# A four-block decoder in one launch: VectorE's links, biases, divisions and norms given to ScalarE and GpSimd, and the first entry's keys sent another way

## The chip, the cores and the metric

The kernel runs on one core of a Trainium2 chip. A core has TensorE (matrix multiplication, PE in the profile, with PEld for its weight loads), VectorE (DVE), ScalarE (ACT), GpSimd (POOL) and SyncE (SP), which here issues nearly all DMAs. The metric is the device time of one execution, in microseconds. Three runs of the kernel before gave 2719.85, 2715.16 and 2719.38 us; their median is 2719.38.

## The reference

Four sequences of 512 rows by 128 features go through twelve layers, each followed by an addition and a layer norm. Every block is a self-mixing layer, an attention across to a context of 154 rows, and a feed-forward layer.

```python
def _layernorm(x, axis=-1, eps=1e-05):
    m = jnp.mean(x, axis=axis, keepdims=True)
    v = jnp.var(x, axis=axis, keepdims=True)
    return (x - m) / jnp.sqrt(v + eps)

x = _layernorm(x + L0_attn(x))            # 16 heads of 8, rotary positions, biases
x = _layernorm(x + L0_xattn(ctx, x))      # own layer norm inside, gamma, beta, biases
x = _layernorm(x + L0_ffn(x))
x = _layernorm(x + L1_attn(x))            # a state scan
x = _layernorm(x + L1_xattn(x, ctx, ctx, mask))
x = _layernorm(x + L1_ffn(x))             # mixture of experts
x = _layernorm(x + L2_attn(x))            # causal attention
x = _layernorm(x + L2_xattn(x, ctx, ctx)) # no mask, biases
x = _layernorm(x + L2_ffn(x))
x = _layernorm(x + L3_attn(x))            # 16 heads of 8, no biases
x = _layernorm(x + L3_xattn(x, ctx, ctx, mask))
x = _layernorm(x + L3_ffn(x))
```

Each attention is the usual one:

```python
scores = jnp.einsum('bhqd,bhkd->bhqk', q, k) / jnp.sqrt(jnp.float32(d_k))
p = jax.nn.softmax(scores, axis=-1)
x = jnp.einsum('bhqk,bhkd->bhqd', p, v)
```

## The kernel before

**Attention with two passes over the scores.** The layers L0_attn and L3_attn (`self_attention`, L605) and the four cross attentions (`cross_attention`, L815) share a scheme. Scores are first computed with queries on the partitions, and VectorE takes their maxima (L671 in self attention, 128 x 2 from 128 x 1024; L962 in cross attention, 128 x 4 from 128 x 616). GpSimd splits a negated maximum into three bfloat16 parts (`split_maxima`, L493 to L496: four small instructions). TensorE transposes these parts (pmx, L504), and the *link* (L506) puts them into the rows of the query operand that are kept for them. Then the scores are computed again, with keys on the partitions (st at L683, stx at L957): the operand's extra rows subtract the maximum within the multiplication. ScalarE takes exp of them, straight from PSUM (L692, L968), and TensorE multiplies by the values (av, avx). So a unit of four heads goes: scores, maxima, split, pmx, link, scores again, exp, values.

**Operands in parts.** A query or key in float32 is carried as three bfloat16 parts in 64 rows of an operand qP or kP: six blocks of 8 rows for products of parts, and rows for maxima. `send` (L403) makes them: projection on TensorE (ps_proj, L407), bias and scale into `raw` (L409, L411 or L413), split into `part` on GpSimd (L414 to L417), and six writes on SP's queue to an area in HBM, far_q, far_k or far_kc (L421), which spread the parts over the rows. `arrive` (L479) loads the operand from there with two DMAs (L482). `raw` and `part` have one buffer each per pool, so one send follows another through them. Rows from `SLOT` on hold the maxima, and the key's rows there are constants, written once by `other_rows` (L278).

**Who makes a bias.** Self attention's query and key biases go through ScalarE (`scaled_bias`, L411). All other biases go through VectorE (L413), which reads the projection in PSUM: cross attention's keys (128 x 154) and queries (128 x 512).

**The order of the work.** Layers are generators, and a list by hand says after which step of a layer a piece goes (`agenda`). A unit of self attention has eight half steps; the first pass runs LEAD = 6 steps ahead of the second. Queries and keys of the next layer are sent from within the present one, where `new["room"]` is set: after steps with s % 16 in (7, 10, 13), L768. For L0_attn and L3_attn this includes s = 61, near their end, where the query of entry 2 of the following cross attention is sent. The first entry's keys in L0_attn use the same raw and part as its query, VectorE makes their parts, and their writes and loads stand on SP's queue behind those of the query.

**Cross attention.** `step(n)` (L1037) does in order: a half step (scores of unit n + 2, second scores of unit n), `sums(n - 1)`, `link_maxima(n + 1)`, the agenda, another half step, `more_sums(n - 1)`, `left(n)` for the last 26 keys, `split_maxima(n + 2)`. PSUM tiles of one bank (pmx, stx, sl, pto and others) come from one ring of three. L0_xattn is the one with `shuffled`: its output is transposed by VectorE (ot, L1011), divided there (rec, L1013, and zt, L1014), gets the input added and a norm of its own (`inner`, `outer`, L1030), where GpSimd applies gamma, beta and the residual. L1_xattn and L3_xattn have a mask, L0_xattn and L2_xattn have none.

**Norms.** `ln_stats` (L329) takes means and variances on VectorE, `applied` (L344) subtracts and scales with four tensor_scalar of 128 x 128 on VectorE (L346).

Of the kernel before, what the change touches and what calls it, by code (L numbers as in the profile page):

```python
# [21 lines left out]
P = 128  # L22
B, S, D = 4, 512, 128
NT = S // P
# [150 lines left out]
def decoder_kernel(ctx: ExitStack, tc: tile.TileContext, x, ctxT, mask1, mask3, packs, offsets, out, layers):  # L175
# [102 lines left out]
    def other_rows(far, what, n):  # L278
        for r in range(2):
            nc.sync.dma_start(far[r, 48:, :, :], flat[:, what : what + 1, :n].to_broadcast([16, 8, n]))  # L280
# [63 lines left out]
    def applied(dst, ys, n, mv, rs):  # L344
        for t in range(n):
            nc.vector.tensor_scalar(  # L346
                dst[:, t, :], ys[:, t, :], mv[:, t, 0:1], rs[:, t : t + 1], ALU.subtract, ALU.mult
            )
# [43 lines left out]
    def scaled(what, scale, pool, name):  # L392
        if scale == 1.0:
            return what
        t = pool.tile([P, 1], F32, name=name, bufs=1)
        nc.vector.tensor_scalar(t, what, scale, None, ALU.mult)
        return t


    Q_ROWS, K_ROWS = ((0, 1, 3), (3, 2, 2), (4, 1, 1)), ((2, 1, 3), (1, 4, 2), (0, 1, 1))  # L400
    SLOT = 48

    def send(far, order, w, rhs, scale, bias, raw, part, scaled_bias=None, on=nc.gpsimd):  # L403

        n = rhs.shape[-1]
        pj = psum_t("ps_proj", kind="a" if "a" in ring else "t")
        nc.tensor.matmul(pj[:, :n], lhsT=w, rhs=rhs, start=True, stop=True)  # L407
        if bias is None:
            nc.scalar.activation(raw, pj[:, :n], AF.Copy, scale=scale)  # L409
        elif scaled_bias is not None:  # L410
            nc.scalar.activation(raw, pj[:, :n], AF.Identity, bias=scaled_bias, scale=scale)  # L411
        else:
            nc.vector.tensor_scalar(raw, pj[:, :n], bias, scale, ALU.add, ALU.mult)  # L413
        on.tensor_copy(part[:, 0, :], raw)  # L414
        on.tensor_tensor(raw, raw, part[:, 0, :], ALU.subtract)
        on.tensor_copy(part[:, 1, :], raw)
        on.tensor_tensor(part[:, 2, :], raw, part[:, 1, :], ALU.subtract)  # L417
        for i, (at, by, m) in enumerate(order):
            for r in range(2):
                rows = far[r].rearrange("(s k) p c -> (k p) s c", k=DK)  # L420
                nc.sync.dma_start(  # L421
                    rows[:, at : at + by * (m - 1) + 1 : by, :],
                    part[64 * r : 64 * r + 64, i : i + 1, :].to_broadcast([64, m, n]),
                )
# [41 lines left out]
    class Operands:  # L466
# [12 lines left out]
        def arrive(self, dst, far):  # L479

            for p in (slice(0, 2), slice(2, 8)):
                nc.sync.dma_start(dst[:, p, :], far.rearrange("r q p c -> (r q) p c")[:, p, :])  # L482
# [15 lines left out]
        def link_maxima(self, n):  # L498

            pm = psum_t("pmx", (P, 2, S), BF16, "a")  # L500
            nm = self.nm[n % 2].rearrange("p (t g) k -> p t (g k)", t=NT)
            for i in range(2):
                for qt in range(NT):
                    nc.tensor.transpose(pm[:, i, qt * P : (qt + 1) * P], nm[:, qt, i * P : (i + 1) * P], identb)  # L504
            q = self.q[n // 4 % 2][:, 2 * (n % 4) : 2 * (n % 4) + 2, :]
            nc.vector.tensor_tensor(q, q, pm, ALU.add)  # L506
# [18 lines left out]
    def out_pieces(b, o, w, keep, cur, new, last, split=False):  # L525
# [23 lines left out]
        return [turn_over, times] + finish_pieces(b, ys, new, last, split)  # L549

    def finish_pieces(b, ys, new, last, split=False):
# [3 lines left out]
        def norm():  # L555
            if split:
                applied(xs, ys, NT, *stats)
            else:
                normed(xs, ys, NT, "f")
            if last:  # L560
                nc.sync.dma_start(out[b].rearrange("(t p) d -> p t d", p=P), xs)
# [43 lines left out]
    def self_attention(w, source, q_scale, k_scale, room, keep, pool, cur, new, last):  # L605
# [5 lines left out]
        bqs = scaled(w["bq"], q_scale, pool, "bqs") if "bq" in w else None  # L611
# [5 lines left out]
        def prepare(b):  # L617
# [21 lines left out]
            def queries():  # L639
                far = far_q[cur["index"] % 2][b]  # L640
                if ("q", b) not in cur["sent"]:
                    send(far, Q_ROWS, w["wq"], src, q_scale, bqs, *room_to_send(pool, S), scaled_bias=bqs)
                ops.arrive(m["q"], far)

            def keys():
                if ("k", b) not in cur["sent"]:

                    on = nc.vector if cur["index"] == 0 and b == 0 else nc.gpsimd
                    send(
                        far_k[b], K_ROWS, w["wk"], src, k_scale, w.get("bk"), *room_to_send(pool, S),  # L650
                        scaled_bias=w.get("bk"), on=on,
                    )
# [44 lines left out]
        def sums(s, h):  # L697
# [17 lines left out]
            if kt == NT - 1:  # L715
# [3 lines left out]
                if j == 3:  # L719
                    pieces = out_pieces(b, m["o"], w, keep, cur, new, last, split=True)  # L720
# [40 lines left out]
        for s in range(steps + LAG):  # L761
# [6 lines left out]
            new["room"] = (lambda n: room_to_send(pool, n)) if s % 16 in (7, 10, 13) else None  # L768
# [46 lines left out]
    def cross_attention(w, cur, new, last, room, scale, mask=None, shuffled=False):  # L815
# [179 lines left out]
        def more_sums(n):  # L995
# [18 lines left out]
            nc.vector.tensor_tensor(  # L1014
# [3 lines left out]
            if j == 3:  # L1018
# [9 lines left out]
                def outer():  # L1028
                    applied(ys, zt, NT, *stats)
# [6 lines left out]
        def step(n):  # L1036
# [5 lines left out]
            if 0 <= n + 1 < units:  # L1042
                ops.link_maxima(n + 1)
# [1361 lines left out]
```

## Time and profile before

| What | Value |
|---|---|
| median of three runs | 2719.38 us |
| the profiled execution's own time | 2717.01 us |
| its span, first to last instruction | 2715.2 us |
| mean granted TensorE clock | 0.959 |
| TensorE busy | 2445.9 us, 90% |
| VectorE busy | 1705.6 us, 63% |
| ScalarE busy | 1240.4 us, 46% |
| GpSimd busy | 1043.7 us, 38% |
| the link, L506, 96 times | 65.7 us, 684 ns each |
| a norm's part, L346, 128 x 128, 188 times | 71.4 us, 447 ns each on the mean |

All times in the profile count from the span's start. L0_attn runs to about 250 us, L0_xattn to 365, L1_attn's scan from 580 to 860, L1_xattn to 980, L2_xattn from 1860 to 1960, L3_attn from 2100 to 2306, L3_xattn to 2430. In a line of the groups, the first number after the bar is the sum of busy time in us, the second the mean of one in ns, and behind the second bar stands idle time of the engine before these instructions, with what ended it. In a line of the timeline stand start in us, duration in us, engine, line, operation, output and input, the count, and in brackets the idle time before it and what ended that.

### The profile page before, as it was taken

To read this page: it belongs to the slowest core of one execution; us is meant where nothing else is said; L and a number is where in the kernel's file an instruction comes from. 1 tells how busy PE (TensorE), PEld (TensorE's weight loads), DVE (VectorE), ACT (ScalarE), POOL (GpSimd) and SP (SyncE) were. 2 spreads that over 40 slices of the span, in tenths; PEclk is the share of its full clock that TensorE was granted. 3 is DMA by queue.
4 is the path that set the end of the run, shared out by engine and by line. 5 is a ranking of instruction groups with operands and counts; after the bars stand their busy time and mean duration, and the time that the engine had idled before them with its cause. 6 is when DMAs were issued, how large, how long until landed. Compare 5 with 4: busy or idle time off the path is not lost. (4 is left out here: it accounts for less than half of the span.)

```text
span 2715.2 us, 37944 instructions
## 1 busy us (share of the span) xinstructions
PE 2445.9 (90%) x14378; PEld 1182.6 (44%) x14378; DVE 1705.6 (63%) x2931; ACT 1240.4 (46%) x2509; POOL 1043.7 (38%) x1360
## 2 busy tenths in 40 slices
PE   4897889978877989999999999998988999899998
PEld 1333334433334444444444555554455233446665
DVE  5896951289987665555545555556756887664444
ACT  2775432377642434333233555553543777343221
POOL 3332420167665327555542444443445332320000
PEclk9999999989988999999999999998987899999999
DMA  4422210000002400000000000002102241300000
GB/s 136 133 78 90 69 35 0 0 0 0 1 15 73 148 7 0 1 1 1 1 1 1 15 7 7 13 13 83 39 1 59 75 115 25 129 32 0 5 4 8
DMA packets 75558, 96.39 MB, mean 36 GB/s; under 512 B 23664, under 2 KB 62320, under 8 KB 75376
## 3 DMA queue, kind: packets, MB, share of 16 engines
q1 hardware_dynamic: 75376, 93.98, 11.8%
q8 instruction: 113, 1.85, 0.3%
q14 instruction: 69, 0.57, 0.1%
HBM read 63.92 MB, written 33.49 MB: 36 GB/s over the span
## 5 line engine op out<-in xcount | busy, mean ns | idle before, releaser
L1163 POOL TENSOR_TENSOR pr<-pr,zs 128x1024 f32<-128x1024 f32 x192 | 237.1, 1252 | 235.2 <-DVE zs L1160 204.8
L671 DVE TENSOR_REDUCE top<-sc 128x2 f32<-128x1024 f32 x256 | 300.9, 1215 | 37.7 <-PE sc L667 34.6
L692 ACT ACTIVATE pT<-st 128x512 f32<-128x512 f32 x512 | 275.9, 597 | 97.9 <-PE st L683 95.2
L1154 ACT ACTIVATE pr<-scc,nm 128x256 f32<-128x256 f32 (+3 forms) x384 | 198.3, 526 | 175.0 <-DVE nm L1148 107.0
L1148 DVE TENSOR_REDUCE nm<-scc 128x2 f32<-128x1024 f32 x192 | 153.6, 820 | 155.2 <-PE scc L1136 154.0
L962 DVE TENSOR_REDUCE top<-scx 128x4 f32<-128x616 f32 x256 | 192.1, 793 | 80.3 <-PE scx L949 77.3
L968 ACT ACTIVATE pTx<-stx 128x512 f32<-128x512 f32 x256 | 139.4, 596 | 206.8 <-PE scx L949 140.0
L2136 POOL TENSOR_TENSOR hh<-hh,cs 128x1024 f32<-128x1024 f32 x64 | 149.2, 2353 | 84.5 <-DVE hh L2132 61.0
L1287 DVE TENSOR_TENSOR vtmp<-psve,gm 128x1024 f32<-128x1024 f32 x64 | 78.3, 1224 | 153.0 <-PE psve L1282 59.6
L706 PE MATMUL av<-pT,vbuf 128*32 128x256 f32 x2048 | 162.6, 392 | 7.2 <-ACT avs L510 7.2
L493 POOL CAST nmP<-top 128x16 bf16<-128x16 f32 x96 | 25.8, 268 | 372.7 <-DVE top L962 214.3
L337 POOL TENSOR_TENSOR rsf<-mvf,eps 128x4 f32<-128x4 f32 x48 | 9.8, 204 | 392.8 <-DVE mvf L335 391.9
L1130 PE MATMUL scc<-k,q 64*128 64x512 f32 (+3 forms) x768 | 143.4, 471 | 6.7 <-ACT pr L1154 2.9
L2132 DVE TENSOR_TENSOR_SCAN hh<-da,pb 128x1024 f32<-128x1024 f32 x64 | 142.6, 2269 | 0.0
L1179 PE MATMUL ptc<-ident,pr 128*128 128x128 f32 x960 | 136.8, 280 | 5.7 <-POOL pr L1163 4.1
L667 PE MATMUL sc<-kP,qP 64*128 64x512 bf16 x512 | 106.2, 413 | 37.6 <-DMA kP<-far_k 18.9
L1292 POOL TENSOR_TENSOR vtmp<-vtmp 128x512 f32<-128x512 f32 x60 | 76.2, 1269 | 162.3 <-DVE vtmp L1287 137.8
L2145 PE MATMUL acc<-hh,ident 128*128 128x512 f32 x256 | 134.4, 652 | 1.9 <-DVE yt L2154 1.9
L1282 PE MATMUL psve<-w_L_ffn,xT 128*128 128x512 f32 x256 | 122.7, 603 | 14.4 <-ACT pr L1154 11.2
L1192 PE MATMUL avc<-pT,v 128*64 128x512 f32 (+3 forms) x768 | 131.4, 449 | 0.5 <-DVE pT L1515 0.5
L1325 PE MATMUL yT<-gT,w_L_ffn 128*128 128x512 f32 x256 | 123.2, 604 | 0.0
L1179 PEld LDWEIGHTS ptc<-ident,pr 128*128 128x128 f32 x960 | 103.4, 141 | 44.4 <-issue 26.0
(408 smaller groups left out, 5050.3 us busy)
## 6 DMA issues: line engine op xcount, KB each, us to landing
qP<-far_q SPq DMA_DIRECT2D x24, 768.0 KB, 6.1
w_L_ffn<-in_L_ffn SPq DMA_DIRECT2D x24, 512.0 KB, 8.5
far_q<-part SPq DMA_DIRECT2D x44, 192.0 KB, 2.8
qP<-far_q SPq DMA_DIRECT2D x24, 256.0 KB, 3.8
kP<-far_k SPq DMA_DIRECT2D x8, 768.0 KB, 5.8
far_q<-part SPq DMA_DIRECT2D x44, 128.0 KB, 2.4
kP<-far_kc SPq DMA_DIRECT2D x16, 231.0 KB, 4.8
w_L_attn<-in_L_attn SPq DMA_DIRECT2D x6, 512.0 KB, 6.5
```

What stands on the lines that cost most here:

```text
L671: return lambda: nc.vector.tensor_reduce(top[:, qt, 2 * gp : 2 * gp + 2], sc, AX.X, ALU.max, negate=True)
L692: nc.scalar.activation(pT, st, AF.Exp)
L706: nc.tensor.matmul(m["av"][32 * g : 32 * g + 32, part], lhsT=m["v"][:, kt, 4 * j + g, :], rhs=weights_of[s, g][:, part], start=(kt == 0 an ...
L962: nc.vector.tensor_reduce(ops.maxima(a)[:, 2 * qp : 2 * qp + 2, 2 * gp : 2 * gp + 2].rearrange("p i r -> p r i"), sc, AX.X, ALU.max, negat ...
L968: nc.scalar.activation(pT, st, AF.Exp)
L1130: nc.tensor.matmul(sc[:, r, at : at + n], lhsT=q[rows, qt * P : n], rhs=k[rows, :n], start=(i == 0), stop=False, skip_group_check=True,)
L1148: nc.vector.tensor_reduce(nm[:, i, :], sc[:, :, at : at + (qt + 1) * P], AX.X, ALU.max, negate=True)
L1154: nc.scalar.activation(pr[:, r, at:to], sc[:, r, at:to], AF.Exp, bias=nm[:, i, r : r + 1], accum_out=zs[:, i, r : r + 1],)
L1163: nc.gpsimd.tensor_tensor(pr[:, :, at : at + n], pr[:, :, at : at + n], zs[:, i, :, None].to_broadcast([P, 2, n]), ALU.mult)
L1179: nc.tensor.transpose(pt[:, r, to : to + P], self.pr[u, p][:, r, lo : lo + P], ident)
L2132: nc.vector.tensor_tensor_scan(flat, das[g % 2][:, c].rearrange("p n t -> p (n t)"), pbs[c].rearrange("p n t -> p (n t)"), 0.0, ALU.mult, ...
L2136: nc.gpsimd.tensor_tensor(m["h", j][c], m["h", j][c], m["C", j], ALU.mult)
```

## The change

- **Links.** In cross attention without a mask (L0_xattn, L2_xattn) the link is two copies on ScalarE, of three partitions each, in place of one addition over 128 partitions on VectorE. The operand's rows are put in another order for that (`SLOT` 32, `Q_ROWS`, `K_ROWS`), so that the rows of maxima begin at partitions 32 and 96. The sizes of the writes stay as they are.
- **Biases.** Every `send` with a bias goes through ScalarE; where there is a scale, VectorE scales the bias, a tile of 128 x 1.
- **Division and norms.** zt's multiplication and the inner norm's `applied` in L0_xattn are GpSimd's. So is `applied` in L0_attn and L3_attn, but for the last entry. GpSimd's program in L0_xattn has zt ahead of the split of the step.
- **Sending.** With `s < 60` the query of entry 2 is no longer sent at s = 61 of L0_attn and L3_attn, but within the cross attention that follows, after its step 1.
- **First keys.** The first entry's keys in L0_attn have a pool of their own, so a raw and part of their own; VectorE still makes their parts, and their six writes and two loads are on ScalarE's queue.

```diff
-            nc.sync.dma_start(far[r, 48:, :, :], flat[:, what : what + 1, :n].to_broadcast([16, 8, n]))
+            nc.sync.dma_start(far[r, 32:48, :, :], flat[:, what : what + 1, :n].to_broadcast([16, 8, n]))
...
-    def applied(dst, ys, n, mv, rs):
+    def applied(dst, ys, n, mv, rs, on=nc.vector):
         for t in range(n):
-            nc.vector.tensor_scalar(
+            on.tensor_scalar(
...
-    Q_ROWS, K_ROWS = ((0, 1, 3), (3, 2, 2), (4, 1, 1)), ((2, 1, 3), (1, 4, 2), (0, 1, 1))
-    SLOT = 48
+    Q_ROWS, K_ROWS = ((1, 1, 3), (6, 1, 2), (0, 1, 1)), ((0, 3, 3), (1, 6, 2), (2, 1, 1))
+    SLOT = 32
...
-        elif scaled_bias is not None:
-            nc.scalar.activation(raw, pj[:, :n], AF.Identity, bias=scaled_bias, scale=scale)
         else:
-            nc.vector.tensor_scalar(raw, pj[:, :n], bias, scale, ALU.add, ALU.mult)
+            if scale != 1.0:
+                scaled_bias = small.tile([P, 1], F32, tag="sb", name="sb", bufs=2)
+                nc.vector.tensor_scalar(scaled_bias, bias, scale, None, ALU.mult)
+                bias = scaled_bias
+            nc.scalar.activation(raw, pj[:, :n], AF.Identity, bias=bias, scale=scale)
...
-            nc.vector.tensor_tensor(q, q, pm, ALU.add)
+            if scalar:
+                for at in (SLOT, 64 + SLOT):
+                    nc.scalar.copy(q[at : at + 3], pm[at : at + 3])
+            else:
+                nc.vector.tensor_tensor(q, q, pm, ALU.add)
...
             def keys():
+                if cur["index"] == 0 and b == 0:
+
+                    with tc.tile_pool(name="first", bufs=1, side="right") as first:
+                        send(
+                            far_k[b], K_ROWS, w["wk"], src, k_scale, w.get("bk"), *room_to_send(first, S),
+                            on=nc.vector, by=nc.scalar,
+                        )
+                    ops.arrive(m["k"], far_k[b], by=nc.scalar)
+                    return
                 if ("k", b) not in cur["sent"]:
...
-                    pieces = out_pieces(b, m["o"], w, keep, cur, new, last, split=True)
+                    on = nc.gpsimd if b < B - 1 else nc.vector
+                    pieces = out_pieces(b, m["o"], w, keep, cur, new, last, split=True, on=on)
...
-            new["room"] = (lambda n: room_to_send(pool, n)) if s % 16 in (7, 10, 13) else None
+            new["room"] = (lambda n: room_to_send(pool, n)) if s % 16 in (7, 10, 13) and s < 60 else None
...
-            nc.vector.tensor_tensor(
+            nc.gpsimd.tensor_tensor(
                 m["zt"][:, j, :].rearrange("p (s d) -> p s d", d=DK), ot[:, :, :DK],
...
-                    applied(ys, zt, NT, *stats)
+                    applied(ys, zt, NT, *stats, on=nc.gpsimd)
...
-                ops.link_maxima(n + 1)
+                ops.link_maxima(n + 1, scalar=mask is None)
```

## The prediction

> **What bounds the kernel now.** I read the page's busy shares and its 40 slices first, then the costliest groups with their shapes kept apart, the clock by stage, and last the timeline at the places that the change touches.
>
> ```profile
> PE 2445.9 (90%) x14378; PEld 1182.6 (44%) x14378; DVE 1705.6 (63%) x2931; ACT 1240.4 (46%) x2509; POOL 1043.7 (38%) x1360
> PE 35%; DVE 6%; ACT 3%; POOL 2%; issue 1%; DMA 1%; SPq 0%; POOLq 0%; DVEq 0%; ACTq 0%
> ```
>
> TensorE is busy for 90% of the span, VectorE for 63%. So work taken off VectorE is worth something only in the stretches where VectorE ends last. Periods between two links of maxima (from one transposition of maxima, L504, to the next, on the timeline) show where. In L0_xattn (260 to 357 us) the 15 periods sum to 97.6 us, with VectorE busy for 90.0 and TensorE for 75.8: VectorE is the bound. In L2_xattn (1869 to 1957) they sum to 87.9, with TensorE at 81: TensorE and latency. In L0_attn and L3_attn a period of 11.6 to 12.5 us holds 11 to 12.5 of TensorE and 10.4 to 12.3 of VectorE, nearly a tie, except for four that hold a norm (13.96, 13.64, 13.96, 13.63; VectorE 13.0 to 13.3, TensorE 11.3 to 12.0).
>
> ```profile
> L506 DVE TENSOR_TENSOR qP<-qP,pmx 128x1024 bf16<-128x1024 bf16 x96 | 65.7, 684 | 23.1 <-PE pmx L504 21.2
> L1526 ACT COPY pT<-ptc 128x1024 f32<-128x1024 f32 x32 | 32.7, 1022 | 2.7 <-PE ptc L1179 2.7
> L2048 ACT COPY rest<-px 8x512 f32<-8x512 f32 x4 | 2.3, 576 | 0.0
> L957 PE MATMUL stx<-qP,kP 64*128 64x512 bf16 x256 | 57.6, 394 | 1.8 <-DVE qP L506 0.7 <-DVE xT L327 0.5 <-DVE v L902 0.2
> L1294 POOL TENSOR_TENSOR v<-vtmp 128x128 f32<-128x128 f32 x60 | 27.5, 458 | 4.7
> ```
>
> The link costs VectorE 0.684 us. ScalarE's copy of 1024 elements from PSUM costs 1.022, and eight partitions (576 ns) cost as much per element as 128 (585 for 512 elements in L510).
>
> **The change, part by part.** Signs are after minus before.
>
> *The link on ScalarE in L2_xattn.* One addition becomes two copies of 3 partitions by 1024. Nearest row: 1.022 each; two copies in a row overlap by about 0.1 (two pTx of 597 ns take 1.08 together), so 1.95 in place of 0.69. The timeline of a period with nothing else in it:
>
> ```profile
> 1897.82 0.62 PE L504 MATMUL pmx<-identb,nmP 128*128 128x128 bf16 x8
> 1898.47 0.69 DVE L506 TENSOR_TENSOR qP<-qP,pmx 128x1024 bf16<-128x1024 bf16 x1
> 1898.89 0.70 PE L957 MATMUL stx<-qP,kP 64*128 64x512 bf16 x2
> 1899.22 0.57 PE L949 MATMUL scx<-kP,qP 64*128 64x154 bf16 x6
> 1899.69 1.51 DVE L962 TENSOR_REDUCE top<-scx 128x4 f32<-128x616 f32 x2
> ...
> 1902.23 0.27 POOL L496 TENSOR_TENSOR nmP<-top,nmP 128x16 bf16<-128x16 f32 x1
> 1902.70 0.62 PE L504 MATMUL pmx<-identb,nmP 128*128 128x128 bf16 x8
> ```
>
> pmx stands in a ring of three PSUM banks; the second stx takes the bank that pmx leaves, so it waits for the link; behind it on TensorE stand the scores that the maximum reads; then the maximum (1.51), GpSimd's split (four small instructions, 1.29), the next pmx. This loop is the period of 4.88, and the link lies in it: a link that lasts 1.26 longer makes a period 6.15. Three such periods: +3.8. Three that also make values (more banks per period): +1.0 each, +3.0. Three that are full on TensorE (5.94, 5.90, 5.90) have about half a microsecond of room: +0.65 each, +2.0. Two with statistics, where VectorE (5.84 of 6.18) loses the link's 0.69 and gives some of it back: -0.3 each. Two with a norm +0.2 each, and the first two +0.4 each: +0.6 for these six. Sum +9.4. Ends: +2, if the bank is seldom the last thing waited for (the group of stx waited only 0.7 us for qP in all), and +14, if all of 15 take 0.95 on the mean.
>
> The Trainium skill ("ScalarE: Activation LUTs", Rules for kernel authors) speaks against this edit: elementwise work belongs on VectorE, up to three times faster in bf16. The rows here show 0.684 against 1.022, a factor of 1.5, and 2.9 only because there are two copies. At three times per copy the link would be about 4.0 us and this layer would lose some 30 us (an estimate from that page's factor); the row decides, and the sum goes by it.
>
> *L0_xattn: link, division and the outer norm.* VectorE loses link 0.68, zt 0.29 and four times 0.3 per norm. GpSimd's zt is priced by its multiplication of the same shape, 0.458. But its program puts zt ahead of the split, and zt comes after the reciprocal. In a plain period: pmx at 0, maxima end at 2.45, ot 0.70, rec 0.25, zt 0.46, split 1.30, semaphores 0.3: 5.55, where 4.66 to 4.85 was. Three of those: +2.5. Those in which a further PSUM bank is wanted before the link is done (5.68, 6.51, 6.84) become about 7.5: +3.5. The one with raw and inner statistics (6.78): +0.4. The two with the outer norm: GpSimd takes 1.85 for it, then its three full-width operations 3.45, zt and split: 10.3 with a query in it (+0.7), 7.3 without (-1.3). Two with final statistics, 6.26 to 5.6: -1.3; two with x, 5.88 to 5.7: -0.4. The query of entry 2, which comes into this layer, puts two multiplications (1.12) and 3.5 us of GpSimd here, mostly beside VectorE: +0.6. The first two as they are. Sum +4.8. Lower end -4: all that VectorE loses in the stretches where it ends last, less the half of it that TensorE's 75.8 us take. Upper end +9: every period by 0.6.
>
> *Norms of L0_attn and L3_attn on GpSimd.* Four tensor_scalar of 0.29 (1.15 us) leave periods where VectorE ends last; the bias of xattn's query (0.75) leaves one period in each. The periods then fall to about TensorE's: 13.96 to 12.6, 13.64 to 12.3; the third norm 0.3. Total -2.7 for L0_attn and -2.6 for L3_attn. GpSimd has room there (1 to 9.5 us in each period); the split behind the norm comes up to 1.85 later, but maxima run six half steps ahead. Ends -4 and 0 for each.
>
> *The query of entry 2 leaves the end of L0_attn and L3_attn.*
>
> ```profile
> 242.22 4.68 SPq L421 DMA_DIRECT2D far_q<-part  x6
> 248.64 0.80 SPq L482 DMA_DIRECT2D kP<-far_kc  x2
> 248.91 1.02 DVE L477 MEMSET nmP<- 128x512 uint32 x2 [5.04 <-DMA far_q<-part]
> 254.46 0.69 PE L949 MATMUL scx<-kP,qP 64*128 64x154 bf16 x8 [6.12 <-DMA qP<-far_q]
> ```
>
> SP issues six writes of far_q; the loads of xattn's first operands reuse the space of part and cannot start until those writes have read it, so TensorE waits 6.12 us. Without them the loads wait for the last av, and its end moves by the 1.12 of the projection that has left: issue near 246, -2.5. In L3_attn the same kP load is issued at 2307.19; it would be near 2305, and since L3_xattn is bound by TensorE the 1.12 comes back there: -1.4. Late next is the qP load itself (four loads in 248 to 260 at 257 GB/s). SP moves past the ffn weights' loads with those six writes; those weights are wanted some 100 us later. Ends -4 and 0 for the two together.
>
> *The first entry's keys.*
>
> ```profile
> 14.71 4.41 SPq L421 DMA_DIRECT2D far_q<-part  x6
> 17.85 0.69 ACT L411 ACTIVATE raw<-ps_proj,w_L_attn 128x512 f32<-128x512 f32 x1 [3.84 <-POOL part L417]
> 20.90 0.43 DVE L414 CAST part<-raw 128x512 bf16<-128x512 f32 x1 [14.55 <-DMA far_q<-part]
> 21.66 4.24 SPq L421 DMA_DIRECT2D far_k<-part  x6
> 29.19 0.80 SPq L482 DMA_DIRECT2D kP<-far_k  x2
> 32.49 1.04 PE L667 MATMUL sc<-kP,qP 64*128 64x512 bf16 x4 [17.50 <-DMA kP<-far_k]
> ```
>
> Keys wait for the query's raw, then for its part, then stand behind its writes on SP. With a room of their own raw starts near 15.1, part near 15.8, and writes on ScalarE's queue near 16.3. But in the changed program each of the query's later writes carries a wait for a write of the keys, since the DMAs of both queues take their completion semaphores from one ring. So the query's writes, 14.71 until now, begin near 19.2 (16.3 and the 2.9 that such a write takes to land), last 6.1 until the load is issued (14.71 to 20.78) and 3.8 until it has landed (to 24.61): 29.1, and the query is what comes last. Against 32.49: -3.4, of which I take -3.2, as transfers are busy 0.69 of 15 to 33 us. Ends 0 (the transfers share what they shared) and -5.4 (keys' writes move from 21.66 to 16.3 and nothing else binds). The Trainium skill (its first page, "Trainium Kernel Development and Optimization", Key Constraints) says that queues of several engines run on the same 16 DMA engines and save only issue time: by that alone only part of the 4.41 us of issue could be won.
>
> *Biases on ScalarE elsewhere.* In L1_attn VectorE, whose scans take 2.27 each, loses 2 x 0.75 + 2 x 0.37; ScalarE takes 0.687 and about 0.3 in their place and has room. -1.2; ends -2.2 and +1. In L2_attn, and in masked L1_xattn, which is bound by TensorE: 0, covered by TensorE; +1 if ScalarE, which there feeds TensorE, is late.
>
> **Sum:** 9.4 + 4.8 - 2.7 - 2.6 - 2.5 - 1.4 - 3.2 - 1.2 = +0.6. The profiled execution took 2717.0 us (span 2715.2), the median of the three runs is 2.4 above it. 2717.0 + 0.6, and half of that distance, is 2719.
>
> **Rivals.** *The link is covered (faster).* If the two copies do not hold TensorE, because the bank was free by another way, L2_xattn costs at most 2 and L0_xattn gains its lower end: 2 - 4 - 13.6, about -15 at the most, and -9 with half of L0_xattn's. For it: stx waited only 0.7 us for qP. Against it: in the rows above the stx that needs the bank follows the link within 0.1 us, once in each period. It decides below about 1.2 us for both copies.
>
> *GpSimd becomes L0_xattn's bound (slower).* Place: zt ahead of the split. Price: in the period that starts at 301 VectorE's own zt took 1.36 in place of 0.29 while GpSimd ran L1032; should GpSimd's zt meet the same, 0.9 more in 10 to 12 of 15 periods is +10: total +10.5, 2729. From a zt of about 0.95 on, the total passes +5.4. Against it: VectorE's maxima read PSUM, and GpSimd's 128x128 multiplications held 458 ns over 60 of them.
>
> *The prologue and norms do nothing.* If TensorE's half steps of 1.11 set L0_attn's pace anyway and the query's loads arrive no sooner, -8.5 becomes about -2: total +7, 2725.
>
> **Numbers.** Forecast as summed, within 6 us on either side: 0.45. Link covered: 0.22. GpSimd bound: 0.18. Prologue and norms nothing: 0.15. A measurement here tells about 0.2%, 5.4 us, from no change. Faster by that: all of the second and a part of the first, 0.31; slower: the last two and a part of the first, 0.40; between them 0.29. The range that leaves two in ten out reaches from -13 to +13: 2706 to 2732; the forecast's own is 2713 to 2725.
>
> **What would show it.** Right: two ScalarE copies near 1.0 us between pmx and the second stx; L2_xattn's plain periods near 6.1 and its 15 periods near 97; L0_xattn's near 102, with GpSimd's split starting after zt; first sc near 29; TensorE's wait for L0_xattn's qP below 4; periods with a norm in L0_attn near 12.5. Wrong: plain periods of L2_xattn still at 4.9, first sc at 32 or at 27, zt on GpSimd near 1.3, or a POOL norm that makes L0_attn's split late.

## The result, and the profile after

The changed kernel takes 2724.85 us (median of 10 runs), the kernel before, beside it, 2718.76 (10 runs). The ratio is 1.003, with a 95% interval of 1.002 to 1.004: slower by some 6 us, where no change beyond the measurement was forecast. The profiled execution of after has a span of 2722.6 us (before 2715.2) and the same mean clock of 0.959.

The page's busy shares and the shares of the chain that ended last, of the kernel after:

```profile
PE 2438.6 (90%) x14378; PEld 1175.7 (43%) x14378; DVE 1660.4 (61%) x2830; ACT 1314.3 (48%) x2597; POOL 1080.4 (40%) x1416
PE 35%; ACT 5%; DVE 4%; POOL 2%; issue 1%; DMA 1%; SPq 0%; POOLq 0%; DVEq 0%; ACTq 0%
```

VectorE lost 45 us of work, ScalarE won 74 and GpSimd 37. On the chain, VectorE went from 6% to 4% and ScalarE from 3% to 5%: the work left VectorE, and ScalarE took its place as the engine waited for.

Where the time went is read by cutting each trace at the start of the transposition of maxima (pmx) that opens each period of an attention layer. The stretches, in us, from one profiled execution of each kernel:

| Stretch | Before | After | Difference | Forecast |
|---|---|---|---|---|
| first scores | 32.5 | 33.6 | +1.1 | -3.2 |
| L0_attn | 200.9 | 199.1 | -1.8 | -2.7 |
| L0_attn's last link to L0_xattn's first | 26.0 | 23.0 | -3.0 | -2.5 |
| L0_xattn, 15 periods | 97.6 | 104.9 | +7.3 | +4.8 |
| L0_ffn and L1_attn | 499.9 | 491.0 | -8.9 | -1.2 |
| L1_xattn | 117.2 | 118.4 | +1.2 | 0 |
| L1_ffn and L2_attn | 894.5 | 901.8 | +7.2 | 0 |
| L2_xattn, 15 periods | 87.9 | 96.2 | +8.3 | +9.4 |
| L3_attn, to L3_xattn, and L3_xattn | 325.8 | 323.8 | -2.0 | -4.0 |
| L2_ffn, and from the last link to the end | 432.9 | 430.9 | -2.0 | 0 |

The last row holds nothing that was changed; its second part is 282.3 or 283.9 to 284.3 in every kernel of this study, so a difference of 2 there says nothing of the change.

The groups of the link, of stx and of GpSimd's new work in after, shapes kept apart (busy us, mean ns, idle time ahead and what ended it):

```profile
L503 ACT COPY qP<-pmx 3x1024 bf16<-3x1024 bf16 x64 | 64.3, 1004 | 46.3 <-PE pmx L499 42.1 <-DMA w_L_ffn<-in_L_ffn 3.9
L960 PE MATMUL stx<-qP,kP 64*128 64x512 bf16 x256 | 58.7, 393 | 18.5 <-ACT qP L503 16.6 <-DVE xT L327 0.5 <-ACT pTx L971 0.2
L346 POOL TENSOR_SCALAR ys<-zt,mvi,rsi 128x128 f32<-128x128 f32 x16 | 12.5, 795 | 0.1
L1017 POOL TENSOR_TENSOR zt<-ot,recx 128x128 f32<-128x128 f32 x16 | 6.5, 406 | 30.8 <-DVE recx L1016 30.7
```

Three partitions by 1024 cost ScalarE 1.00 us, as 128 partitions did before (1.02, L1526, in float32). stx, which had waited 0.7 us in all for a link, now waits 16.6. A plain period of L2_xattn shows where, on the timeline of after:

```profile
1902.91 0.62 PE L499 MATMUL pmx<-identb,nmP 128*128 128x128 bf16 x8
1903.57 2.02 ACT L503 COPY qP<-pmx 3x1024 bf16<-3x1024 bf16 x2 [0.35 <-PE pmx L499]
1903.99 0.38 PE L960 MATMUL stx<-qP,kP 64*128 64x512 bf16 x1
1905.64 0.37 PE L960 MATMUL stx<-qP,kP 64*128 64x512 bf16 x1 [1.28 <-ACT qP L503]
1906.12 1.51 DVE L965 TENSOR_REDUCE top<-scx 128x4 f32<-128x616 f32 x2 [1.52 <-PE scx L952]
1908.65 0.27 POOL L491 TENSOR_TENSOR nmP<-top,nmP 128x16 bf16<-128x16 f32 x1
```

The first stx is made at once, the second waits 1.28 us for the bank that the link still reads, and the scores and maxima behind it start that much later. The period is 6.21 us where it was 4.88.

### The profile page after: what moved, and what is told of

Its sections match the earlier page's. It is cut to its first block, busy times and chain, and to the rows that moved or that the text cites. A ratio compares the mean times of both kernels' runs of the same rounds, so it can differ in the third digit from the quotient of the medians.

```text
span 2722.6 us, 38048 instructions
## 1 busy us (share of the span) xinstructions
PE 2438.6 (90%) x14378; PEld 1175.7 (43%) x14378; DVE 1660.4 (61%) x2830; ACT 1314.3 (48%) x2597; POOL 1080.4 (40%) x1416
## 3 DMA queue, kind: packets, MB, share of 16 engines
q8 instruction: 113, 1.85, 0.3%
## 5 line engine op out<-in xcount | busy, mean ns | idle before, releaser
L488 POOL CAST nmP<-top 128x16 bf16<-128x16 f32 x96 | 25.4, 264 | 342.5 <-DVE top L965 189.8
```

## Experiments

Each kernel was timed beside the kernel before on the same chip (medians of that: 2717.9, 2719.1, 2719.2 and 2718.3, in the order of the experiments). The profiles are read by the stretches of the table. Most periods that are the same work in two kernels agree within some hundredths of a microsecond. These places vary more among kernels that do the same there, and differences below that are not read from single runs: the first five periods of L0_attn (periods 2 and 4, counted from 0, by some 3 us either way; GpSimd's parts wait there for transfers), the first two periods of the cross attentions and L1_xattn's fourth (by about 1) and fifth (by 1.6), the way from L3_attn to L3_xattn (24.6 to 26.2), the stretch with L1_attn (by up to 6) and that with L2_attn (by 4). The first scores came at 32.5 to 33.8 in the four kernels with the first keys as before, and at 33.6 to 34.5 in the four with two queues.

The granted TensorE clock differs too in some short stretches. In L0_xattn's ninth period the same work took 5.34 us at a granted clock of 1.00 and 6.95 at 0.55, and in its two periods of 5.88 in the kernel before the clock was 0.75. Where single periods of cross attention are set against each other below, the clock is 0.95 or more in both, or it is given. Between 15 and 45 us it was 0.5 to 0.6 in after and 1.00 in before; but in the kernel of the first experiment, which does the same there as after, it was 1.00 and the first scores came at 34.3, so it is not what delayed them.

### The link back on VectorE

```diff
-                ops.link_maxima(n + 1, scalar=mask is None)
+                ops.link_maxima(n + 1)
```

> The changed kernel with the link of L0_xattn and L2_xattn on VectorE again (one addition over 128 partitions), all else as changed. In the trace of after the 15 periods of L2_xattn sum to 96.2 us (87.9 before) and those of L0_xattn to 104.9 (97.6 before). Theory A, the link's length lies on the loop through PSUM's ring in both layers: L2_xattn comes back to 88 (-8.3), L0_xattn gives back the part that the bank's wait makes, about 4 (to about 101), and the whole run is near 2712 to 2714 us. Rival B, in L0_xattn GpSimd's division ahead of the split is the whole loss: L2_xattn -8.3 all the same, but L0_xattn stays at 105 or rises by up to 2, since VectorE has 15 times 0.68 us more; whole run near 2717.

Measured: 2725.79 us, 1.0026 (1.0016 to 1.0036) against before. L2_xattn came back to 87.9, every period to within 0.04 of its old length. L0_xattn rose from 104.9 to 108.1. So theory A holds in L2_xattn and fails in L0_xattn, where rival B holds and is too mild: with GpSimd's division in place, VectorE's link makes the layer longer still. By periods it is mixed: one with values fell (7.34 to 6.57), one with a final norm rose (5.55 to 6.42). The one with final statistics ahead of it rose from 5.34 to 7.39, but at a granted clock of 0.60 against 1.00, so that its size is not the link's alone. The net -5 of the two layers does not show in the time, which had been expected at 2712 to 2714; the stretches with L1_attn and L2_attn, which this edit leaves alone, came out 2.9 and 2.4 longer than in the profile of after, and the end 1.7.

### Division and inner norm back on VectorE

```diff
-            nc.gpsimd.tensor_tensor(
+            nc.vector.tensor_tensor(
                 m["zt"][:, j, :].rearrange("p (s d) -> p s d", d=DK), ot[:, :, :DK],
...
-                    applied(ys, zt, NT, *stats, on=nc.gpsimd)
+                    applied(ys, zt, NT, *stats)
```

> The changed kernel with the division (zt) and the inner norm's subtraction and scaling of L0_xattn on VectorE again. L0_xattn's periods sum to 104.9 in after. If GpSimd's place in the chain is what costs (four tensor_scalar of 128x128 took 3.13 us there, and the split waited for zt): the two periods with the outer norm lose 1.5 to 3 each (11.99 and 9.11 now), plain ones 0 to 0.5 (5.34 now, 4.66 before), sum near 99, run near 2719. If the link on ScalarE is what costs: at most -2, near 103. L2_xattn stays at 96.2 either way.

Measured: 2717.55 us, 0.9997 (0.9988 to 1.0006): level with before. L0_xattn fell by 8.4 to 96.5, more than was expected, and below the 97.6 of before, although the link stays on ScalarE and a query is made in the layer. GpSimd was the bound there, not only in the periods with the inner norm: those with inner statistics and with values fell too (7.62 to 5.99 and 7.34 to 6.39). The timeline of after for the period that begins at 302.1, GpSimd's instructions and the next pmx:

```profile
301.96 0.61 POOL L409 CAST part<-raw 128x512 bf16<-128x512 f32 x1
302.64 1.15 POOL L410 TENSOR_TENSOR raw<-raw,part 128x512 f32<-128x512 f32 x1
303.86 0.61 POOL L411 CAST part<-raw 128x512 bf16<-128x512 f32 x1
304.55 1.15 POOL L412 TENSOR_TENSOR part<-raw,part 128x512 bf16<-128x512 f32 x1
305.69 3.13 POOL L346 TENSOR_SCALAR ys<-zt,mvi,rsi 128x128 f32<-128x128 f32 x4
308.90 1.10 POOL L1033 TENSOR_TENSOR ys<-ys,w_L_xattn 128x512 f32<-128x512 f32 x1
310.07 1.09 POOL L1034 TENSOR_TENSOR ys<-ys,w_L_xattn 128x512 f32<-128x512 f32 x1
311.24 1.26 POOL L1035 TENSOR_TENSOR ys<-ys,x 128x512 f32<-128x512 f32 x1
312.46 0.40 POOL L1017 TENSOR_TENSOR zt<-ot,recx 128x128 f32<-128x128 f32 x1
...
314.10 0.62 PE L499 MATMUL pmx<-identb,nmP 128*128 128x128 bf16 x8 [4.19 <-POOL nmP L491]
```

GpSimd is busy without a gap from 302 to 314: the query's parts, the norm at 3.13, three full-width operations, the division, and only then the split. TensorE waits 4.19 us for it. The period took 11.99 (clock 0.86); with the two operations back on VectorE it took 8.92 (0.97).

### Cross attention's biases back on VectorE

```diff
+        elif vec:
+            nc.vector.tensor_scalar(raw, pj[:, :n], bias, scale, ALU.add, ALU.mult)
         else:
...
-                    far_kc[b], K_ROWS, w["wk"], ctx_sb[:, b, :], 1.0, w.get("bk"), *room(KC)
+                    far_kc[b], K_ROWS, w["wk"], ctx_sb[:, b, :], 1.0, w.get("bk"), *room(KC), vec=True,
...
-                    far_q[i % 2][b], Q_ROWS, w["wq"], x_T[:, b, :], scale, w.get("bq"), *room(S)
+                    far_q[i % 2][b], Q_ROWS, w["wq"], x_T[:, b, :], scale, w.get("bq"), *room(S), vec=True,
```

> The changed kernel with the biases of cross attention's keys and queries on VectorE again (those of L0_attn stay on ScalarE). The aligned traces of before and after show three stretches that only these instructions can explain: L1_attn's scan, where after wins about 11 us between 784 and 830 us, L1_xattn's third period (+1.1), and L2_attn, where after loses about 8 between 1500 and 1862. Theory: all three come back: L1_attn's scan +10.5, L1_xattn -1.1, L2_attn -7 to -8.5; the sum of these is +1 to +2.5, and the run is near 2727. Rival: the win or the loss comes from something else in the run (a transfer, the clock): then one of the stretches stays as in after, and the run moves by 7 or more.

Measured: 2732.61 us, 1.0052 (1.0037 to 1.0067). All three stretches went back: L1_attn's +11.3 (502.3), L2_attn's -7.0 (894.8), L1_xattn's -0.9. The run came 5.6 above the 2727 that was expected, and it moved by 7.8 against after, which the rival had named as its sign; but no stretch stayed. L0_attn became 3.4 longer, 3.0 of it in period 4 (20.19 against 17.18), block 3 2.4 and the end 1.7, all places that vary, so this surplus is left open. The biases are one edit with two large effects of opposite sign.

The loss, on the timelines of L2_attn around one key, first before:

```profile
1501.23 0.38 DVE L413 TENSOR_SCALAR raw<-ps_proj,w_L_xattn 128x154 f32<-128x154 f32 x1 [0.99 <-PE ps_proj L407]
1502.10 1.02 ACT L1526 COPY pT<-ptc 128x1024 f32<-128x1024 f32 x1
1502.23 0.31 POOL L414 CAST part<-raw 128x154 bf16<-128x154 f32 x1
1504.15 3.03 POOL L1163 TENSOR_TENSOR pr<-pr,zs 128x768 f32<-128x768 f32 x3
1507.07 1.09 PE L1179 MATMUL ptc<-ident,pr 128*128 128x128 f32 x8
```

and after:

```profile
1496.89 1.02 ACT L1529 COPY pT<-ptc 128x1024 f32<-128x1024 f32 x1
1497.79 0.42 ACT L408 ACTIVATE raw<-ps_proj,w_L_xattn 128x154 f32<-128x154 f32 x1
1498.28 0.31 POOL L409 CAST part<-raw 128x154 bf16<-128x154 f32 x1 [1.20 <-ACT raw L408]
1500.01 3.03 POOL L1166 TENSOR_TENSOR pr<-pr,zs 128x768 f32<-128x768 f32 x3
1503.10 0.44 PE L1182 MATMUL ptc<-ident,pr 128*128 128x128 f32 x2 [0.34 <-POOL pr L1166]
```

On ScalarE the bias stands behind its row of exps and the copy of pT. So the key's parts start later on GpSimd, the scaling of weights (pr) behind them too, and TensorE, which had waited for nothing there, waits for pr. Against this experiment's trace each of the four keys costs 0.6 us and the three queries 1.1, 2.8 and 1.1. TensorE's waits for pr add up to 8.9 us between 1480 and 1862 in after, to 4.1 in before and to 4.2 here. So they show 4.8 of the 7; where TensorE loses the rest was not traced.

### The first keys on SP's queue

```diff
-                            on=nc.vector, by=nc.scalar,
+                            on=nc.vector,
...
-                    ops.arrive(m["k"], far_k[b], by=nc.scalar)
+                    ops.arrive(m["k"], far_k[b])
```

> The changed kernel with the first keys' six writes and two loads on SP's queue again, behind those of the query; their own raw and part stay. In after the first scores start at 33.63 us, in before at 32.49. Theory: the query's writes wait for the keys' writes in after, through completion semaphores taken in turn, and with one queue they start at 14.7 again, the keys' writes follow at about 19.2 in place of 21.7: first scores at 30.0, 3.6 earlier than after and 2.5 earlier than before, run near 2721. Rival: the transfers' own rate sets the end (they were busy 0.69 of 15 to 33 us before): first scores stay at 32.5 or later, run 2723 to 2725.

Measured: 2727.98 us, 1.0038 (1.0023 to 1.0053); first scores at 34.4 us. The theory's first half holds: the query's writes begin at 14.99 again, while in after SP had waited 5.5 us for the keys' writes, in four waits. Its second half fails, and not only by the transfers' rate: the keys' writes were issued at 22.1, since on one queue they stand behind the query's loads (issued at 21.2), and they then took 4.9 to 6.7 us to land beside these loads of 1 MB (4.1 to 5.7 in before, with the same order). The 34.4 lies among the 33.6 to 34.5 of the kernels with two queues, so it is no better than they, and not worse.

### The parts mixed

The changed kernel with the division and inner norm, L2_xattn's link and L2_xattn's biases on VectorE, and the first keys as in the kernel before:

```diff
-                ops.link_maxima(n + 1, scalar=mask is None)
+                ops.link_maxima(n + 1, scalar=shuffled)
...
-                    far_kc[b], K_ROWS, w["wk"], ctx_sb[:, b, :], 1.0, w.get("bk"), *room(KC)
+                    far_kc[b], K_ROWS, w["wk"], ctx_sb[:, b, :], 1.0, w.get("bk"), *room(KC), vec=name == "L2_xattn",
```

> From the changed kernel: L0_xattn's division and inner norm on VectorE; L2_xattn's link on VectorE (L0_xattn's stays on ScalarE); L2_xattn's biases on VectorE (all others stay on ScalarE); the first entry's keys as in the kernel before, sharing raw, part and SP's queue with the query. Norms on GpSimd and the query of entry 2 stay as changed. Theory, each part owes what the single runs showed: against after, L0_xattn -8.4 (96.5), L2_xattn -8.3 (88), L1_ffn and L2_attn -8 (894 to 896), first scores at 32.5 in place of 33.6: sum -25, so 2700 us, 18 below before. Rival: the parts hide one another's waits, and less than half comes through: 2708 to 2714.

Measured: 2699.25 us, 0.9923 (0.9909 to 0.9937). L0_xattn 94.7, L2_xattn 87.5, the stretch with L2_attn 892.5, first scores at 33.0. The parts add up as their single runs said; the rival falls.

### The mix, with L0_xattn's link on VectorE too

```diff
-                ops.link_maxima(n + 1, scalar=shuffled)
+                ops.link_maxima(n + 1, scalar=False)
```

> The mixed kernel (division, inner norm, L2_xattn's link and biases on VectorE, first keys as before) with L0_xattn's link on VectorE too. It tells whether a plain period of L0_xattn has two chains of the same length in after (5.34 us with the link on ScalarE, 5.39 with GpSimd's division alone): with both gone it must fall to 4.66 as before. Expected: plain periods 4.66, those with statistics back at 6.2 to 6.8, L0_xattn 96 to 99 in all, run within 3 us of the mixed kernel. Rival: one of the two alone set the 5.34 and the plain periods stay at 5.3.

Measured: 2702.79 us, 0.9935 (0.9921 to 0.9949); L0_xattn 95.8. The plain periods fell to 4.66, as expected. So after had two chains of nearly the same length there: 5.39 with GpSimd's division alone, 5.34 with ScalarE's link alone, 5.34 with both. One of them taken away shows nothing. With inner statistics or a final norm beside it, ScalarE's link was the shorter (6.00 against 6.52, 5.34 against 5.68).

### All writes ahead of all loads

The mix, with a raw and part of the keys' own, on SP's queue, against the changed kernel:

```diff
             def queries():
...
+                if cur["index"] == 0 and b == 0:
+                    return
                 ops.arrive(m["q"], far)
...
-                            on=nc.vector, by=nc.scalar,
+                            on=nc.vector,
...
-                    ops.arrive(m["k"], far_k[b], by=nc.scalar)
+                    ops.arrive(m["q"], far_q[0][b])
+                    ops.arrive(m["k"], far_k[b])
                     return
```

> The mixed kernel, but the first entry's keys have a raw and part of their own, everything on SP's queue, and in the order: the query's six writes, the keys' six writes, then the loads of both. With the query's loads ahead of the keys' writes the first scores came at 34.4 in the run with one queue, and the keys' writes took 6 to 7 us to land beside those loads (2.8 for the query's). Theory, order on the queue sets it: keys' writes at 19.5 to 23.8, landed by 26.5, first scores at 30.3; 2 us below the mixed kernel. Rival, the transfers' rate sets it: 32 or later, same as the mixed kernel.

Measured: 2693.89 us, 0.9907 (0.9893 to 0.9921); first scores at 30.6, 2.4 earlier than in the mix. The rest of the 5.4 us between the two medians is not located; the two profiled executions differ by 2.2. The first transfers on the timeline of after:

```profile
16.16 5.19 ACTq L416 DMA_DIRECT2D far_k<-part  x6
19.14 5.84 SPq L416 DMA_DIRECT2D far_q<-part  x6
23.94 0.86 ACTq L477 DMA_DIRECT2D kP<-far_k  x2
30.11 0.83 SPq L477 DMA_DIRECT2D qP<-far_q  x2
33.63 1.04 PE L669 MATMUL sc<-kP,qP 64*128 64x512 bf16 x4 [18.81 <-DMA qP<-far_q]
```

and of this kernel:

```profile
15.66 3.89 SPq L418 DMA_DIRECT2D far_q<-part  x6
19.64 3.88 SPq L418 DMA_DIRECT2D far_k<-part  x6
23.62 1.02 SPq L479 DMA_DIRECT2D qP<-far_q  x2
25.05 0.79 SPq L479 DMA_DIRECT2D kP<-far_k  x2
30.64 1.04 PE L674 MATMUL sc<-kP,qP 64*128 64x512 bf16 x4 [15.47 <-DMA kP<-far_k]
```

With two queues the query's writes began at 19.14, 3 us behind the keys', and the last of them were under way together with the keys' loads (issued at 23.94); the query's load could be issued only at 30.11. In one queue, with writes first, both loads are out by 26.

### The query of entry 2 sent where it was

```diff
-            new["room"] = (lambda n: room_to_send(pool, n)) if s % 16 in (7, 10, 13) and s < 60 else None
+            new["room"] = (lambda n: room_to_send(pool, n)) if s % 16 in (7, 10, 13) else None
```

> The mixed kernel with the query of entry 2 sent at s = 61 of L0_attn and L3_attn again. Read by stretch. Theory: from the last link period of L0_attn to L0_xattn's first +3 (23 to 26), in L3_attn +1.3 (24.9 to 26.2), and L0_xattn and L3_xattn get back what the query costs there: L3_xattn -1 (one period 7.53 to 6.58), L0_xattn -0.5 to -2; run +1 to +3. Rival: what it costs in L0_xattn is as much as it wins ahead of it; run within 1.

Measured, once: 2702.66 us. Against the mix, the way from L0_attn to L0_xattn grew by 2.3 (25.4), that from L3_attn to L3_xattn by 1.9 (26.5); L3_xattn's period fell from 7.53 to 6.58, and L0_xattn stayed at 94.8: the query is free there. (The first periods of L0_attn came out 3 longer, in places that vary.) In block 0 the way took 23.0 to 23.9 in all twelve kernels with the query moved, and 26.0 and 25.4 in the two without, so the edit is worth some 2.3 there. In block 3 it shows no gain: the way and L3_xattn together take 138.2 to 140.8 in the twelve, 139.1 on the mean, and 138.6 and 139.6 in the two.

### Links by period

```diff
-                ops.link_maxima(n + 1, scalar=shuffled)
+                ops.link_maxima(n + 1, scalar=shuffled and not 2 <= n + 1 <= 5)
```

> The kernel with the reordered first transfers, but in L0_xattn the links of units 2 to 5 are on VectorE and the others on ScalarE. By period, VectorE's link was the shorter choice there (5.18, 5.58, 4.66, 4.66 against 5.99, 6.39, 5.34, 5.34), ScalarE's in the periods with statistics and norms. Theory, the link's engine acts period by period: those four fall by 0.7 to 0.8 each, L0_xattn near 93, run 3 us below the one with reordered transfers (2691). Rival: a period takes over what the last one left, and the win stays under 1.5.

Measured: 2693.17 us, 0.9909 (0.9892 to 0.9925). The four periods fell to 5.17, 5.58, 4.66 and 4.66, and L0_xattn to 92.8; two periods behind them gave 0.8 of it back (6.00 to 6.51, 8.93 to 9.19). Net 2.2 us by these six periods; the time, 0.7 below the kernel with reordered transfers, does not tell the two apart. The rival's bound of 1.5 is passed by the periods, so the link's engine acts nearly period by period.

### L1_xattn's own biases on VectorE

```diff
-        how = {what: f for _, what, f in sends(cur["index"], cur["xT"])}
+        how = {what: f for _, what, f in sends(cur["index"], cur["xT"], mask is not None)}
```

> As the kernel with mixed links, and the biases that L1_xattn sends for itself are on VectorE again (those sent from L1_attn stay on ScalarE). L1_xattn's fourth period was 8.77 before, 9.66 to 10.04 with ScalarE's biases and 9.01 with VectorE's. Theory: it falls to about 8.9, L1_xattn by 0.7 to 1, run within 1 of 2690. Rival: the period depends on the state of the transfers, and it stays at 9.7.

Measured: 2689.78 us, 0.9896 (0.9881 to 0.9911), the fastest of the study, 29 us below before. The period went from 9.50 to 9.02; it takes 9.50 to 10.34 in the ten kernels with ScalarE's biases there and 8.77 to 9.02 in the four with VectorE's. L1_xattn as a whole moved by 0.3 only, and the profiled executions of the two kernels differ by as much; the 3.4 us between their medians is not located.

### Norms back on VectorE

```diff
-                    on = nc.gpsimd if b < B - 1 else nc.vector
+                    on = nc.vector
```

> The kernel with the reordered first transfers, with the norms of L0_attn and L3_attn on VectorE again. Theory: the four periods with a norm go back from 12.93, 12.61, 12.93, 12.61 to 13.96, 13.64, 13.96, 13.63 (+4.1 in all), and the third norms by under 0.1 each; run +4. Rival: TensorE sets these periods by now, under +1.

Measured, once: 2699.30 us. The four periods went back to 13.96, 13.64, 13.96 and 13.63, as expected, +4.1 in all against the kernel with reordered transfers (2693.89). Periods 3 and 4 of L0_attn, which the edit does not touch, were 2.1 longer as well.

### Only the biases that fall into the scan

The fastest kernel, with the biases that L1_attn sends for L1_xattn on VectorE (the query's line changes in the same way):

```diff
-                    far_kc[b], K_ROWS, w["wk"], ctx_sb[:, b, :], 1.0, w.get("bk"), *room(KC), vec=vec or name == "L2_xattn",
+                    far_kc[b], K_ROWS, w["wk"], ctx_sb[:, b, :], 1.0, w.get("bk"), *room(KC), vec=vec or name in ("L1_xattn", "L2_xattn"),
```

> The fastest kernel so far, with one thing put back: the biases of the keys and queries that L1_attn sends for L1_xattn are on VectorE again. It isolates the stretch that the sum of the prediction priced at -1.2. Theory: a bias that falls between two products of the scan's loop puts VectorE out of step with TensorE for the steps that follow, so that the stretch from L0_xattn's last link to L1_xattn's first gets 10 to 12 us longer (489 to about 500) and the run is near 2700. Rival: VectorE just loses the time of these instructions, 2 x 0.75 + 2 x 0.37: +2, run near 2692.

Measured: 2701.41 us, 0.9945 (0.9928 to 0.9961). The stretch went from 488.8 to 499.9, which is before's length. The theory holds: four instructions of 2.3 us in all cost 11. In this trace VectorE stands idle for 6.2 us ahead of them, and for 4.1 us ahead of products where it had stood 1.2. The timeline of before, VectorE's scan and what interrupts it:

```profile
786.17 0.38 DVE L413 TENSOR_SCALAR sq<-ps_proj,w_L_xattn 128x154 f32<-128x154 f32 x1 [2.80 <-PE ps_proj L407]
788.73 4.46 DVE L2132 TENSOR_TENSOR_SCAN hh<-da,pb 128x1024 f32<-128x1024 f32 x2
793.10 1.21 DVE L2129 TENSOR_TENSOR pb<-du,pb 128x1024 f32<-128x1024 f32 x1
795.72 1.23 DVE L2129 TENSOR_TENSOR pb<-du,pb 128x1024 f32<-128x1024 f32 x1 [1.41 <-PE pb L2104]
796.86 4.46 DVE L2132 TENSOR_TENSOR_SCAN hh<-da,pb 128x1024 f32<-128x1024 f32 x2
```

and of after:

```profile
796.38 2.33 DVE L2132 TENSOR_TENSOR pb<-du,pb 128x1024 f32<-128x1024 f32 x2
798.62 4.46 DVE L2135 TENSOR_TENSOR_SCAN hh<-da,pb 128x1024 f32<-128x1024 f32 x2
803.04 2.35 DVE L2132 TENSOR_TENSOR pb<-du,pb 128x1024 f32<-128x1024 f32 x2
805.30 4.46 DVE L2135 TENSOR_TENSOR_SCAN hh<-da,pb 128x1024 f32<-128x1024 f32 x2
```

Without a bias, VectorE runs two products and two scans back to back, 6.62 us in a step of this part. With one, it first waits 2.80 us for the projection, which TensorE makes in its own time, and afterwards it comes to some products before TensorE has made their operand (1.41 us of waiting in the step shown). The last six steps of before took 9.81, 8.13, 9.40, 7.90, 8.43 and 8.18 from scan to scan, those of after 6.62 or 6.68.

## Why the prediction was wrong

No change beyond the measurement was forecast (+0.6 as summed), and the kernel became 6 us slower. Two steps made the total wrong: GpSimd's price for the inner norm in L0_xattn, and the time that the first query's writes take until its load can be issued. Two more, both on biases, were each wrong by some 7 us and hid each other.

**The link in L2_xattn: right.** +9.4 was said and +8.3 measured; the loop through PSUM's ring, the two copies (1.95 said, 2.02 measured) and the plain period (6.15 said, 6.21 measured) are there. The terms of single periods fit less well: the first two fell by 0.5 together where +0.8 was said. The rule of the Trainium skill ("ScalarE: Activation LUTs", Rules for kernel authors), that elementwise work belongs on VectorE, names the right engine for this layer; its factor of up to about three, which it gives for operations with one source, was 1.5 here, between one copy on ScalarE and an addition on VectorE.

**L0_xattn: right in sign, its GpSimd term too small.** +4.8 was said and +7.3 measured. The step that failed is "GpSimd takes 1.85 for" the inner norm. It was priced from a multiplication (0.458), and four tensor_scalar took 3.13 (0.78 each, where the group's mean is 0.795). The period said to be 10.3 took 11.99. The other one, said to be 7.3, took 9.11, at a granted clock of 0.63 (8.33 at 1.00 in two other kernels with the same work there). The plain period was 5.34 (5.55 said, though the terms listed add up to 5.46), but for two reasons of which one was counted. The two periods of 5.88 that were priced as work had run at a granted clock of 0.75. The Trainium skill ("GPSIMD Engine Reference", section 4.1) has VectorE as about twice as fast for two inputs and GpSimd at roughly line rate for one; measured here at 128 x 128, the operation with two tensor inputs took 0.41 against VectorE's 0.29, a factor of 1.4, and the one with a single tensor and two scalars per row 0.795 against 0.34, a factor of 2.3: the reverse (VectorE's are medians of before).

**The biases: two wrong terms.** "L1_attn -1.2" was -8.9 in the profiles, and -11 where the run on the scan isolates it. The step counted the time of four instructions; it did not ask what VectorE waits for ahead of them, nor what they do to a loop in step with TensorE. "In L2_attn: 0, covered by TensorE" was +7.2, and +8.6 on the mean: 903.3 in the four kernels with ScalarE's biases there (901.8, 902.9, 904.1, 904.5), 894.7 in the ten with VectorE's. The step looked at the engine that takes the work in and not at the queue behind it: ScalarE gives GpSimd its raw later, GpSimd's pr comes later, TensorE waits. The question to ask was: who waits for the moved instruction?

**The first keys: wrong.** -3.2 was said, +1.1 measured, +1.0 between the means of four kernels each. "The query's writes begin near 19.2" was right (19.14). "Last 6.1 until the load is issued" was taken from before, where nothing ran beside them; it took 11.0 (19.14 to 30.11), while the keys' loads went out at 23.94: the six writes took 1.4 longer to issue, and SP then waited 4.9 for them to land where it had waited 1.5. That the keys' loads ran beside them is the likely reason, but it is not shown: no run holds these loads back with two queues. The rule quoted from the Trainium skill, that a second queue saves issue time only, agrees as far as it goes: the second queue won nothing. Order in one queue won 2.4 us against the mix.

**Norms and the query of entry 2: right in kind, too large in part.** The four periods with a norm fell by 1.0 each (1.3 to 1.4 said); L0_attn as a whole changed by -1.8 (-2.7 said), L3_attn by -1.6 (-2.6 said), as the third norms and the bias gave nearly nothing. The query was worth -3.0 in block 0 (-2.5 said). In block 3 it was -1.3 plus 0.95 in these two profiles (-1.4 said in all), and nothing on the mean of all kernels.

**The sum and the rivals.** The two missed bias terms nearly cancel in the profiles (-7.7 and +7.2 off), and so hardly show in the total; that they cancel is luck. The error of the total, +6.8 between the two profiles, is then the first keys (+4.3) and L0_xattn (+2.5), with smaller ones on both sides. "The link is covered" falls with stx's 16.6 us. "GpSimd becomes L0_xattn's bound" was right in its place and wrong in its reason: zt held 0.41 us, the norm and the order did it. "The prologue and norms do nothing" was half right, and its 2725 is by chance what was measured. The stated range held the measured time, but the value forecast, 2719, is level with before, and after is not.

## What to carry to other kernels

Price a moved instruction by the queue that it joins and by who waits behind that queue, not by its duration: four biases of 2.3 us were worth -11 us in one layer, and seven of 3.8 us were worth +7 to +9 in another. An engine's relief pays per stretch, so the choice of engine can be made per stretch: of this change the biases in the scan, the norms and the query's place in block 0 are gains, the division, the inner norm, one layer's link and biases are losses, and the parts added up to 29 us below before once sorted. Where two chains of equal length end together, undoing one of them shows nothing, and both must be taken away before either is judged.

## What the runs showed of the hardware that was not expected

- A copy on ScalarE of 3 partitions by 1024 took as long as one of 128 partitions (1.00 and 1.02 us).
- On GpSimd a tensor_scalar of 128x128 with two operands per row took 0.795 us, nearly twice the 0.406 of a product of two tensors of that size.
- From the first of the query's six writes to its load, 6.1 us went by with one queue, and 11.0 when a second queue's writes and loads of 1 MB ran beside them. With all writes ahead of all loads in a single queue, the first scores, which need both operands, came 3 us earlier than with two (30.6 against 33.6).
- Three biases of 0.4 to 0.75 us on VectorE, in every second of six steps of its scan, made all six longer: 7.9 to 9.8 us, and 7.9 to 8.2 in those that held none, where a step without them takes 6.6.
